# A group norm of the next layer computed inside attention windows: another form of it in the first layer, an earlier table of gather places, a later load of scan weights

## The chip, the core and the metric

The kernel runs on one core of a Trainium2 chip. The metric is the device time of one execution in microseconds (us). A core has five engines that run side by side and wait for each other by semaphores: PE (TensorE, matrix products), DVE (VectorE), ACT (ScalarE), POOL (GpSimd) and SP (SyncE, which here only issues transfers). Each engine takes its own instructions strictly in order. Transfers that SP and ACT issue run on 16 DMA engines. The profile also gives the clock that TensorE was granted, as a share of full speed.

## The reference

The input is a batch of 4 images of 256 channels on 64 x 64 places. Four layers follow each other, each of the form x = x + layer(gn(x)). The norm is `_gn`:

```python
g = v.reshape(B_, H_, W_, G, C_ // G)
m = jnp.mean(g, axis=(1, 2, 4), keepdims=True)
s = jnp.var(g, axis=(1, 2, 4), keepdims=True)
return ((g - m) / jnp.sqrt(s + eps)).reshape(v.shape)
```

It is called with x itself, so its last axis is the last image axis. With 64 places there and 32 groups, a group is two neighbouring columns of the image over all channels and rows. Layers 0 and 1 are the attention layers that this change touches. Each has two halves:

```python
y = mhsa(x, ...)          # 1x1 convolutions, tanh, then a recurrence h = f*h + (1-f)*z along one axis
return ssa(y_img, ...)    # attention in 8 x 8 windows
```

In `ssa`, each of the 64 windows of 64 places picks the four windows whose mean key fits its mean query best (`top_k`), takes their keys and values (`kv[idx]`), and attends to those 256 places with 8 heads. A 3 x 3 depthwise convolution of the values is added, and a 256 x 256 projection closes the layer. Layers 2 and 3 are state-space layers and are not touched.

## The kernel before, in words

The outer loop runs over the 4 images. For each, `attention_layers` runs layers 0 and 1, and two other functions run layers 2 and 3. The image x stays in SBUF as 128 partitions x (2 halves of the channels x 64 x 64 places). A strip is 8 columns of it, so there are 8 strips and each strip holds 4 norm groups.

Each attention layer has a scan phase and a window phase. **The scan phase** (`scan_phase`) goes through the 8 strips: it normalises a strip two strips ahead with `gn_four`, convolves, runs the recurrence, and stores keys and values of the strip to a table in DRAM (`kv_dram`; the values by `kv_dram<-vn`, L394, are the last part). It needs the layer's scan weights `att_wa` (1 MB, L115), and strips 0 and 1 must be normalised before it begins: for layer 1 that is done during the window phase of layer 0. `routing` then computes the four places of each window; the instruction on L472 writes them to the tile `idx`, which is the start of the window phase in this document.

**The window phase** (`window_phase`) takes the 64 windows in 32 pairs. There are 8 window phases in a run: images 0 to 3, and for each layer 0 and layer 1. Pair i goes through these steps:

- `gather(i)` fetches keys and values of the pair's 8 places by 8 transfers of 128 KB (L524). SP issues them, but ACT issues half of those of pairs 0 and 1. The buffers `kv` hold four pairs; `gather(i + 3)` stands at the end of pair i, after `values(i - 1)` has freed buffers.
- `indices(i)` loads the places into registers of the issuing engine: for pairs 0 to 3 straight from `idx` (L511, one load a window), for later pairs from `row` (L501, one load a pair).
- `load_row` stores `idx` to DRAM (`listed<-idx`, L493) and, when the store has landed, reads it back into one partition as `row` (L494). It stands behind `gather(2)` and `indices(3)`.
- `scores(i, h)` for h = 0, 1 (half of the heads) is 64 small products on PE (L546). `smallest` is a DVE reduction (L558), `exps` four ACT exponentials with their sums (L569), `normalise` a DVE reciprocal (L581) and four POOL multiplications of 128 x 256 (L584).
- `turn` transposes the result on PE (L597), `turned` copies it out on DVE and ACT (L608, L610), `values` multiplies with the values (L623), and `own_rows(i)` adds into the image of the convolution on DVE (L634). L634 runs once a pair, so its starts are used as marks of the pairs below.
- In two of four pairs the projection of the strip before is added to x (L644).

Other work is spread over the pairs by hand. `taps` are the last steps of the depthwise convolution on POOL, one a pair until pair 24: a multiplication into a tile `tap` (L254), then an addition (L257), in turn. `double` sends part of the queries to other partitions by SP (L309). Then there is the norm. The function `plan` puts its steps either into `mids[i]` (in the middle of pair i, ahead of `normalise(i, 0)`) or into `ends[i]` (at the end of pair i, behind everything else of it).

In layer 0 the steps are those of `gn`, for strips 0 and 1 of the next layer, begun at pairs 7 and 11:

1. `sums`, DVE, end of pair 7 (11), L143, and a product on PE at the end of pair 8 (12);
2. `center`, middle of pair 9 (13): the mean on DVE (L149), then POOL writes x minus the mean into `att_xn`, 128 x 1024 (L151);
3. `square`, ACT, end of pair 10 (14): L156, into the tile `gn_sq`, which has the tag "sq" with one buffer, and that is also the buffer of `tap`;
4. `reduce`, DVE, middle of pair 11 (15), L160, and a product at the end of it;
5. `scale`, middle of pair 12 (16): DVE adds the epsilon (L167), POOL raises to the power of minus a half (L168), and POOL multiplies `att_xn` by that, 128 x 1024 (L172).

In layer 1 the next layer needs only variances, so the steps are those of `stats`, for strips 0 to 6, begun at pairs 7, 11, 15 and so on: `sums` (L200), `mean` (L206), four ACT squares of 128 x 256 straight from x with mean and sum in the same instruction (L215, into a tile of the tag "xn"), a product, and `variance`, a DVE copy (L221).

`load_scan_weights(nxt)` stands, in layer 0, ahead of the loop over the pairs and behind `load_row`, in SP's order between `gather(2)` and `gather(3)`.

Of the kernel before, what the change touches and what calls it, by code (L numbers as in the profile page):

```python
# [8 lines left out]
F32 = mybir.dt.float32  # L9
# [3 lines left out]
ALU = mybir.AluOpType  # L13
# [5 lines left out]
P = 128  # L19
# [4 lines left out]
NW = 8  # L24
# [20 lines left out]
class Net:  # L45
# [33 lines left out]
    def attention_layers(self, x, w_drams, v_drams):  # L79
        tc, nc = self.tc, self.nc  # L80
        with ExitStack() as ctx:
# [31 lines left out]
            def load_scan_weights(lay):  # L113
                lay["wa"] = wp.tile([P, 2, 4 * C], F32, tag="wa", name="att_wa")
                nc.sync.dma_start(lay["wa"], lay["w"][:, :, 0 : 4 * C])  # L115
# [70 lines left out]
                return g[0], both(g[1], g[2]), both(g[3], g[4]), both(g[5], g[6])  # L186


            def stats(s, psum):
                xs = x.rearrange("p (c h w) -> p c w h", c=2, w=S)[:, :, strip[s], :]  # L190
                box = {}

                def columns(tag, part):
                    box[tag] = psum().tile([P, NT], F32, tag="mm", name=f"gn_{tag}")
                    nc.tensor.matmul(box[tag][:, 0:4], self.one_gn, part, start=True, stop=True)

                def sums():
                    box["s1"] = self.small.tile([P, 4], F32, tag="gn_s1", name="gn_s1")
                    xr = x.rearrange("p (n w) -> p n w", w=S)[:, :, strip[s]]
                    nc.vector.tensor_reduce(  # L200
                        box["s1"], xr.rearrange("p n (g t) -> p g n t", t=2), AX.XY, ALU.add
                    )

                def mean():
                    box["mean"] = self.small.tile([P, 4], F32, tag="gn_mean", name="gn_mean")
                    nc.vector.tensor_scalar(  # L206
                        box["mean"], box["pm"][:, 0:4], -1.0, None, ALU.mult
                    )

                def square(g):  # L210
                    if g == 0:
                        box["s2"] = self.small.tile([P, 4], F32, tag="gn_s2", name="gn_s2")
                        box["sq"] = norm.tile([P, 2, 8, S], F32, tag="xn", name="gn_sq")
                    two = slice(2 * g, 2 * g + 2)
                    nc.scalar.activation(  # L215
                        box["sq"][:, :, two], xs[:, :, two], AF.Square,
                        bias=box["mean"][:, g : g + 1], accum_out=box["s2"][:, g : g + 1],
                    )

                def variance():  # L220
                    nc.vector.tensor_copy(self.gvar[:, 4 * s : 4 * s + 4], box["pv"][:, 0:4])  # L221

                return (
                    sums, lambda: columns("pm", box["s1"]), mean,
                    *(lambda g=g: square(g) for g in range(4)),
                    lambda: columns("pv", box["s2"]), variance,
                )


# [247 lines left out]
            def window_phase(lay, work, psum, idx, nxt, taps):  # L477
                vec, wb = lay["vec"], lay["wb"]
                n_pair = NW * NW // 2
# [11 lines left out]
                def load_row():  # L491
                    listed = dram.tile([NW * NW, 8], U32, tag="listed", name="listed")
                    nc.sync.dma_start(listed, idx)  # L493
                    nc.sync.dma_start(  # L494
                        row.rearrange("o (s a) k -> o s a k", a=NW),
                        listed[:, 0:TOPK].rearrange("(o a s) k -> o s a k", o=1, a=NW),
                    )

                def indices(i):
                    if 3 < i < n_pair:  # L500
                        loads, win = nc.values_load_multi_w_load_instructions(  # L501
                            row[0:1, 2 * i : 2 * i + 2, :], engines=[ET.SP], min_val=0,
                            max_val=NW * NW - 1,
                            skip_runtime_bounds_check_because="places among 64 columns",
                        )
                        regs[i] = [win[0:TOPK], win[TOPK:]]
                    elif i < n_pair:
                        regs[i] = []
                        for w in range(2):
                            p = window(i, w)  # L510
                            loads, win = nc.values_load_multi_w_load_instructions(  # L511
                                idx[p : p + 1, 0:TOPK], engines=[queue(i, w)[1]], min_val=0,
                                max_val=NW * NW - 1,
                                skip_runtime_bounds_check_because="places among 64 columns",
                            )
                            regs[i].append(win)
# [121 lines left out]
                def project(s, m, psum):  # L638
# [10 lines left out]
                    return add  # L649

                indices(0)
                for i in range(3):
                    gather(i)
                    indices(i + 1)
                load_row()
                scores(0, 0)
                scores(0, 1)
                early = [query(lay, 5, m, psum, nc.vector, tag="pt", bufs=2) for m in range(2)]
# [5 lines left out]
                mids, ends, left = {}, {}, []  # L664

                def plan(steps, *where):
                    for f, (at, i) in zip(steps, where):
                        if i < n_pair:
                            at.setdefault(i, []).append(f)
                        else:  # L670
                            left.append(f)

                if nxt:
                    load_scan_weights(nxt)
                    for s in range(2):
                        i = 7 + 4 * s
                        plan(gn(nxt, s, lambda: psum), (ends, i), (ends, i + 1), (mids, i + 2),
                             (ends, i + 3), (mids, i + 4), (ends, i + 4), (mids, i + 5))
                else:

                    for s in range(NW - 1):
                        i = 4 * s + 7
                        plan(stats(s, lambda: psum), (ends, i), (ends, i + 1), (mids, i + 2),
                             (ends, i + 2), (mids, i + 3), (ends, i + 3), (mids, i + 4),
                             (ends, i + 4), (mids, i + 5))
                for i in range(n_pair):
                    sj, a = divmod(i, 4)
                    add = evict = None
                    exps(i, 0, (0, 1))
                    if i:  # L690
                        scores(i, 1)
                        turned(0, 0)
                        turned(0, 1)
                        turn(i - 1, 1)
                        smallest(i, 1)
                    exps(i, 0, (2, 3))
                    for t in mids.get(i, ()):
                        t()
                    if i == 0:
                        for f in early:  # L700
                            f()
                    normalise(i, 0)
                    if a == 3 and sj + 2 in (NW - 2, NW - 1):
                        evict = query(lay, sj + 2, 0, psum)
                    elif a == 0 and sj + 1 in (NW - 2, NW - 1):
                        evict = query(lay, sj + 1, 1, psum)
                    elif a in (1, 2) and sj:
                        add = project(sj - 1, a - 1, psum)
                    exps(i, 1, (0, 1))
                    scores(i + 1, 0)  # L710
                    if i:
                        turned(1, 0)
                        turned(1, 1)
                        values(i - 1)
                    turn(i, 0)
                    smallest(i + 1, 0)
                    exps(i, 1, (2, 3))
                    normalise(i, 1)
                    if i:
                        own_rows(i - 1)  # L720
                    for t in taps[i : i + 1]:
                        t()
                    if a in (0, 3) and i and dve_taps:
                        dve_taps.pop(0)()
                    if add:
                        add()
                    if evict:
                        evict()
                    gather(i + 3)
                    if a == 0 and 1 < sj + 1 < NW - 2:  # L730
                        double(sj + 1)
                    elif a == 1 and sj + 1 in (NW - 2, NW - 1):
                        double(sj + 1)
                    indices(i + 4)
                    for t in ends.get(i, ()):
                        t()
                turned(0, 0)
# [14 lines left out]
                box = {}  # L752
# [3 lines left out]
            with tc.tile_pool(name="at_p0", bufs=2, space=PSUM, reuse_waits="tile") as psum:  # L756
                box = {"psum": psum}
                g = [gn_four(layers[0], s, lambda: box["psum"]) for s in range(2)]
# [1413 lines left out]
```

## Time and profile before

| what | value |
|---|---|
| median of the runs | 11914.07 us (3 runs, 11912.61 to 11917.38) |
| the profiled execution | 11903.13 us, of which the span from first to last instruction 11901.3 us |
| PE busy | 10069.9 us, 85% |
| DVE busy | 9868.8 us, 83% |
| POOL busy | 8695.6 us, 73% |
| ACT busy | 7006.9 us, 59% |
| mean granted TensorE clock | 0.932 |
| the 8 window phases, end of the last instruction on L472 to the start of the last L634 | 274.2, 271.1, 268.1, 270.1 us in layer 0; 243.7, 245.1, 251.6, 252.6 us in layer 1 |

Busy shares over the whole span say little here, since some two thirds of the time lie in layers 2 and 3. What matters is where the window phases of layer 0 and of layer 1 differ. They do the same attention, in the same order; beside it they carry different norm work and, in layer 0, the weight load. The stretches that the next sections use are cut at starts of L634: "pair 9 to pair 16" is from its run for pair 9 to its run for pair 16.

### The profile page before, as it was taken

To read this page: it belongs to the slowest core of one execution; us is meant where nothing else is said; L and a number is where in the kernel's file an instruction comes from. 1 tells how busy PE (TensorE), PEld (TensorE's weight loads), DVE (VectorE), ACT (ScalarE), POOL (GpSimd) and SP (SyncE) were. 2 spreads that over 40 slices of the span, in tenths; PEclk is the share of its full clock that TensorE was granted. 3 is DMA by queue.
4 is the path that set the end of the run, shared out by engine and by line. 5 is a ranking of instruction groups with operands and counts; after the bars stand their busy time and mean duration, and the time that the engine had idled before them with its cause. 6 is when DMAs were issued, how large, how long until landed. Compare 5 with 4: busy or idle time off the path is not lost. (4 is left out here: it accounts for less than half of the span.)

```text
span 11901.3 us, 192225 instructions
## 1 busy us (share of the span) xinstructions
PE 10069.9 (85%) x71104; PEld 5762.7 (48%) x71104; DVE 9868.8 (83%) x8422; ACT 7006.9 (59%) x13096; POOL 8695.6 (73%) x5918
## 2 busy tenths in 40 slices
PE   8998887777899888777789988877778998887777
PEld 4564454444456455444445645544444564554444
DVE  6677998998767799899866779989987677998998
ACT  4565554776456555577645655557764565555776
POOL 4566886898456688689845668868984566886897
PEclk9998998999999899899999989989999998998998
DMA  3344454554334455455433445545543344554554
GB/s 96 101 133 137 173 178 144 171 181 159 89 99 137 138 172 175 147 169 181 157 88 101 133 139 172 176 147 169 181 158 92 98 134 139 173 175 145 169 175 154
DMA packets 682505, 1742.09 MB, mean 146 GB/s; under 512 B 88896, under 2 KB 194896, under 8 KB 681312
## 3 DMA queue, kind: packets, MB, share of 16 engines
q1 hardware_dynamic: 676448, 1721.41, 44.7%
q8 instruction: 563, 9.22, 0.3%
q10 hardware_dynamic: 5120, 8.39, 0.3%
q14 instruction: 374, 3.06, 0.1%
HBM read 1601.52 MB, written 94.39 MB: 142 GB/s over the span
## 5 line engine op out<-in xcount | busy, mean ns | idle before, releaser
L1016 POOL TENSOR_TENSOR hc<-h,cb 128x1024 f32<-128x1024 f32 x2056 | 4807.7, 2350 | 785.6 <-DVE h L1010 341.4
L1010 DVE TENSOR_TENSOR_SCAN h<-da,m_state,pb 128x1024 f32<-128x1024 f32 x1248 | 2920.2, 2340 | 163.1 <-DVE pb L1004 4.3
L962 PE MATMUL y<-ident,hc 128*128 128x128 f32 x16384 | 2345.2, 290 | 404.4 <-POOL hc L1016 333.7
L962 PEld LDWEIGHTS y<-ident,hc 128*128 128x128 f32 x16384 | 2043.7, 150 | 1127.6 <-POOL hc L1016 575.0
L1004 DVE TENSOR_TENSOR pb<-du,pb 128x1024 f32<-128x1024 f32 x1672 | 2024.4, 1211 | 118.9 <-PE pb L934 116.8
L946 ACT ACTIVATE da<-delta,m_v 128x1024 f32<-128x1024 f32 x1672 | 1899.4, 1141 | 135.7 <-DVE h L1010 118.9
L934 PE MATMUL pb<-m_parts,pick 128*128 128x512 bf16 x3312 | 1081.8, 411 | 835.0 <-DVE h L1010 768.7
L584 POOL TENSOR_SCALAR pr<-pr,sm,zero 128x256 f32<-128x256 f32 x2048 | 1136.1, 569 | 533.6 <-DVE sm L581 530.2
L569 ACT ACTIVATE pr<-sc,mn 128x256 f32<-128x256 f32 x2048 | 952.7, 477 | 552.4 <-DVE sm L581 359.9
L934 PEld LDWEIGHTS <-pick 128*128 128x128 bf16 x3312 | 264.0, 101 | 1779.8 <-DVE h L1010 977.2
L558 DVE TENSOR_REDUCE mn<-sc 128x4 f32<-128x1024 f32 x512 | 629.6, 1231 | 528.3 <-PE sc L546 527.0
L1010 DVE TENSOR_TENSOR_SCAN h<-da,pb 128x1024 f32<-128x1024 f32 x424 | 969.3, 2286 | 55.6 <-ACT m_u L1704 0.5
L920 POOL TENSOR_TENSOR bb<-du,bb 128x1024 f32<-128x1024 f32 x376 | 888.5, 2363 | 118.7 <-DMA bb<-m_cd 108.3
L597 PE MATMUL pt_ps<-ident,pr 128*128 128x128 f32 x4096 | 663.9, 297 | 85.0 <-POOL pr L584 40.2
L1010 DVE TENSOR_TENSOR_SCAN h<-dap,m_state,bb 128x1024 f32<-128x1024 f32 x288 | 672.2, 2334 | 65.9 <-ACT dap L946 46.1
L233 PE MATMUL conv_ps<-att_y,att_wb 128*128 128x512 f32 x1536 | 686.7, 597 | 3.0 <-DVE gvar L221 3.0
L546 PE MATMUL sc<-kv,q_swap 32*64 32x128 f32 x8192 | 599.4, 286 | 11.4 <-DMA kv<-kv_dram 8.8
L946 ACT ACTIVATE dap<-delta,m_v 128x1024 f32<-128x1024 f32 x376 | 419.8, 1116 | 308.5 <-DVE h L1010 245.8
L546 PE MATMUL sc<-kv,att_y 32*64 32x128 f32 x7168 | 580.1, 287 | 17.4 <-DMA kv<-kv_dram 13.7
L597 PEld LDWEIGHTS pt_ps<-ident,pr 128*128 128x128 f32 x4096 | 471.5, 148 | 225.6 <-POOL pr L584 138.4
L271 DVE SCALAR_TENSOR_TENSOR lp<-vimg,att_v,lp 128x512 f32<-128x512 f32 x672 | 507.7, 755 | 30.8 <-DVE lp L271 1.0
L546 PEld LDWEIGHTS sc<-kv,att_y 32*64 32x64 f32 x7168 | 434.0, 139 | 153.3 <-issue 58.8
(300 smaller groups left out, 17799.4 us busy)
## 6 DMA issues: line engine op xcount, KB each, us to landing
cb<-m_cd SPq DMA_DIRECT2D x2048, 512.0 KB, 3.8
kv<-kv_dram SPq DMA_DIRECT2D x1984, 128.0 KB, 2.8
bb<-m_cd SPq DMA_DIRECT2D x376, 512.0 KB, 5.5
kv_dram<-kst SPq DMA_DIRECT2D x128, 256.0 KB, 3.9
kv_dram<-vn SPq DMA_DIRECT2D x128, 256.0 KB, 4.1
q_swap<-att_y SPq DMA_DIRECT2D x96, 256.0 KB, 4.4
m_pe<-in_pe_dram SPq DMA_DIRECT2D x32, 512.0 KB, 4.5
out_dram<-yo SPq DMA_DIRECT2D x64, 256.0 KB, 2.4
```

The costliest lines, as they stand in the source:

```text
L233: nc.tensor.matmul(ps, w[:, k, w0 + m * P : w0 + (m + 1) * P], src[:, k], start=(k == 0), stop=(k == 1),)
L546: nc.tensor.matmul(sc[h][b * 64 : b * 64 + 64, r, w, m, :], (own(sj, m) if r == b else swap[sj % 2][:, m])[rows, 2 * a + w], kv[i, w][rows ...
L569: nc.scalar.activation(t[:, g].rearrange("p j r t -> p r j t"), sc[h][:, :, g // 2, g % 2, :].rearrange("p r (j t) -> p r j t", j=2), AF.E ...
L584: nc.gpsimd.tensor_scalar(t[:, g], t[:, g], s[:, g : g + 1], self.zero, ALU.mult, ALU.add)
L597: nc.tensor.transpose(pt[h][j][:, g, :], t[:, g, j].rearrange("p r t -> p (r t)"), self.ident,)
L920: nc.gpsimd.tensor_tensor(pb[i], slots[i][0]["du"], pb[i], ALU.mult)
L934: nc.tensor.matmul(pb[i][:, ss], self.pick[:, n : n + 1].to_broadcast([P, P]), blk["parts"][:, ss], start=True, stop=True,)
L946: nc.scalar.activation(da[i], blk["delta"], AF.Exp, scale=blk["a"](n))
L962: nc.tensor.matmul(blk["y"][:, ss], t[:, ss], self.ident, is_transpose=True, start=(n == 0 and ss.start % NT == 0), stop=(n == DS - 1 and ...
L1004: nc.vector.tensor_tensor(pb[i], blk["du"], pb[i], ALU.mult)
L1010: nc.vector.tensor_tensor_scan(h[i][:, ss], da[i][:, ss], pb[i][:, ss], state, ALU.mult, ALU.add)
L1016: nc.gpsimd.tensor_tensor(hc[i][:, ss], h[i][:, ss], cb[i][:, ss], ALU.mult)
```

## The change

It has three parts.

1. In layer 0 too, the norm of the next layer's strips 0 and 1 takes the steps of `stats`. Two steps are new: `deviation` (middle of pair 12 and 16) adds the epsilon on DVE and raises to the power on POOL, for 4 columns instead of 8; `scale`, twice, at the ends of pairs 13 and 14 (17 and 18), makes two POOL instructions of 128 x 256 each, (x + (minus mean)) * deviation, reading x and writing the tile that held the squares. That tile becomes `att_xn`. The steps of `gn` stay in use in the scan phases.
2. `load_row` moves ahead of `gather(0)`, in all 8 window phases, and pairs 2 and 3 take their places from `row` too.
3. `load_scan_weights(nxt)` moves to the end of pair 4, behind `gather(7)`, the query transfers (`double`) and `indices(8)`. In SP's order it is then directly ahead of `gather(8)`.

```diff
-            def stats(s, psum):
+            def stats(s, psum, lay=None):
...
                         box["sq"] = norm.tile([P, 2, 8, S], F32, tag="xn", name="gn_sq")
+                        if lay:
+                            lay["xn"][s] = box["sq"]
...
+                def deviation():
+                    rstd = self.small.tile([P, 8], F32, tag="gn_rstd", name="gn_rstd")
+                    box["rstd"] = rstd = rstd[:, 0:4]
+                    nc.vector.tensor_scalar(rstd, box["pv"][:, 0:4], 1e-5, None, ALU.add)
+                    nc.gpsimd.tensor_tensor(
+                        rstd, rstd, self.minus_half.to_broadcast([P, 4]), ALU.pow
+                    )
+
+                def scale(*gs):
+                    for g in gs:
+                        two = slice(2 * g, 2 * g + 2)
+                        nc.gpsimd.tensor_scalar(
+                            box["sq"][:, :, two], xs[:, :, two], box["mean"][:, g : g + 1],
+                            box["rstd"][:, g : g + 1], ALU.add, ALU.mult,
+                        )
...
-                    lambda: columns("pv", box["s2"]), variance,
+                    lambda: columns("pv", box["s2"]),
+                    *((deviation, lambda: scale(0, 1), lambda: scale(2, 3)) if lay else (variance,)),
...
-                    if 3 < i < n_pair:
+                    if 1 < i < n_pair:
...
                 indices(0)
+                load_row()
                 for i in range(3):
                     gather(i)
                     indices(i + 1)
-                load_row()
...
-                if nxt:
-                    load_scan_weights(nxt)
-                    for s in range(2):
-                        i = 7 + 4 * s
-                        plan(gn(nxt, s, lambda: psum), (ends, i), (ends, i + 1), (mids, i + 2),
-                             (ends, i + 3), (mids, i + 4), (ends, i + 4), (mids, i + 5))
-                else:
...
+                for s in range(2 if nxt else NW - 1):
+                    i = 4 * s + 7
+                    plan(stats(s, lambda: psum, nxt), (ends, i), (ends, i + 1), (mids, i + 2),
+                         (ends, i + 2), (mids, i + 3), (ends, i + 3), (mids, i + 4),
+                         (ends, i + 4), (mids, i + 5), (ends, i + 6), (ends, i + 7))
...
                     indices(i + 4)
+                    if i == 4 and nxt:
+                        load_scan_weights(nxt)
```

## The prediction

> **What bounds the kernel now.** I read the page first, then the sums by stretch for all 8 window phases, then the order of time of single engines. The page shows no engine that is full everywhere, so the stage decides. The change touches window phases alone, and layer 1 already does the norm in nearly the form that layer 0 is to get: it is the control. These are the sums by stretch from pair 9 to pair 16. The columns are start and end, length, the busy time of PE, weight load, DVE, ACT and POOL with counts, granted clock, DMA share and GB/s; first the four phases of layer 0, then the four of layer 1.
> ```profile
> 315.31:388.71 73.40, 62.42 (x1028) 47.31 (x1027) 40.39 (x63) 35.85 (x128) 48.43 (x68) 0.70 0.42 123
> 3283.76:3358.27 74.51, 65.73 (x1029) 50.12 (x1027) 39.83 (x64) 35.96 (x128) 48.52 (x68) 0.63 0.43 125
> 6260.69:6331.88 71.19, 57.31 (x1028) 43.43 (x1027) 40.94 (x63) 35.73 (x128) 48.33 (x68) 0.78 0.46 133
> 9232.42:9304.15 71.73, 57.83 (x1028) 43.57 (x1027) 40.56 (x63) 35.74 (x128) 48.33 (x68) 0.79 0.41 119
> 778.21:827.59 49.38, 46.86 (x1030) 34.93 (x1029) 38.35 (x63) 38.32 (x138) 38.85 (x63) 1.00 0.57 159
> 3745.38:3795.73 50.35, 47.09 (x1030) 35.91 (x1029) 38.46 (x64) 38.33 (x138) 38.84 (x63) 0.97 0.56 159
> 6725.88:6774.94 49.06, 45.42 (x1030) 34.35 (x1029) 38.44 (x64) 38.22 (x138) 38.85 (x63) 1.00 0.58 166
> 9694.36:9745.19 50.83, 47.57 (x1030) 36.09 (x1029) 38.27 (x63) 38.43 (x138) 38.82 (x63) 0.97 0.54 159
> ```
> The same seven pairs take 290.8 us in layer 0 and 199.6 in layer 1. No engine of layer 0 has 20 us more to do; POOL has 9.6 more. The rest is waiting, and a PE at 0.63 to 0.79 of its clock. In layer 1 PE is busy 95% of the stretch: there it is the bound. The order of time says where layer 0 waits, for ACT at pair 10, and for POOL at pair 12:
> ```profile
> 318.85 1.06 ACT L156 ACTIVATE gn_sq<-att_xn 128x1024 f32<-128x1024 f32 x1 [4.89 <-POOL vimg L257]
> ```
> ```profile
> 330.81 1.64 POOL L168 TENSOR_TENSOR gn_rstd<-gn_rstd,minus_half 128x8 f32<-128x8 f32 x1 [1.61 <-DVE sm L581]
> 332.53 1.90 POOL L172 TENSOR_TENSOR att_xn<-att_xn,gn_rstd 128x1024 f32<-128x1024 f32 x1
> 334.42 4.74 POOL L584 TENSOR_SCALAR pr<-pr,sm,zero 128x256 f32<-128x256 f32 x8
> ```
> First, the square waits 4.89 us until POOL's addition L257 has read `tap`: both tiles share the one buffer of the tag "sq". Behind the square stand all exponentials of the next pair. Second, power and multiplication (1.64 + 1.90) stand ahead of eight normalisations whose sums were ready. Both leave PE without transposes.
>
> The early part, pair 0 to pair 9, in the same columns: layer 0, then the first two phases of layer 1 (the other two took 67.52 and 64.55).
> ```profile
> 246.03:315.31 69.28, 63.72 (x1317) 48.43 (x1318) 45.62 (x74) 43.68 (x162) 51.13 (x82) 0.90 0.59 169
> 3215.72:3283.76 68.04, 62.23 (x1317) 46.62 (x1318) 45.45 (x73) 43.69 (x162) 51.19 (x82) 0.95 0.58 168
> 6195.40:6260.69 65.29, 60.54 (x1317) 45.41 (x1318) 45.28 (x73) 43.42 (x161) 50.63 (x82) 0.97 0.56 160
> 9162.23:9232.42 70.19, 63.55 (x1317) 48.34 (x1318) 45.48 (x74) 43.69 (x162) 51.13 (x82) 0.90 0.61 174
> 717.44:778.21 60.77, 57.30 (x1317) 43.12 (x1317) 45.53 (x73) 45.37 (x167) 48.22 (x81) 1.00 0.60 173
> 3684.03:3745.38 61.35, 58.43 (x1317) 43.55 (x1318) 45.24 (x73) 45.55 (x168) 48.66 (x81) 1.00 0.60 174
> ```
> Layer 0 loses 272.8 - 4 x 61.1 = 28.4 us here. Its cause shows on SP and PE in the first phase:
> ```profile
> 240.02 0.48 SPq L493 DMA_DIRECT2D listed<-idx  x1
> 241.69 0.82 SPq L494 DMA_DIRECT2D row<-listed  x1
> 242.57 0.40 SPq L115 DMA_DIRECT2D att_wa<-in_l_w_dram  x1
> ```
> ```profile
> 251.54 0.40 PE L546 MATMUL sc<-kv,att_y 32*64 32x128 f32 x2 [2.38 <-DMA kv<-kv_dram]
> ```
> `gather(3)` goes out behind store, readback and the 1 MB of weights, and its scores wait.
>
> **The norm.** Removed for each strip: POOL's L151 (2.47 us), L172 (1.90) and the power on 8 columns (1.64), DVE's reduction (1.22), one ACT square (1.06), and with them both stalls. Added: four ACT squares of 0.75 with 0.21 to read the sum, 3.84 in all; layer 1 carries exactly these at the same pairs, so they cost nothing beyond its stretch. The squares' tile has the tag "xn", so the 4.89 us wait goes away. If only the control's steps were left, layer 0 would gain 91.2 us. What the control lacks is `deviation` and `scale`.
>
> `deviation`: the DVE addition replaces a copy of 0.14 in the same place, no change. The power stands ahead of pair 12's normalisation on POOL, and behind it wait the normalisations, the tap and PE's transposes. In the control POOL begins that normalisation at 788.70, 0.15 after the deviation would be there, and ends at 790.86; the transposes start at 791.01. So of 1.64 us (the row of 8 columns; fewer columns may take less), 1.64 - 0.15 - 0.15 = 1.34 reach PE. The low end is 0.7, if the power is a third shorter and is partly caught up.
>
> `scale`: two POOL instructions at each of two pair ends. The contiguous form (L584, 128 x 256) takes 0.57. But x is read here at a step of 64 floats. The Trainium skill ("GPSIMD Engine Reference", section Performance pitfalls for Q7 kernels) says that a POOL read at a step over 8 bytes costs some 2.9 instead of 1.9 cycles an element; at its 1.2 GHz that is an estimate of 0.57 + 256 x 1.0/1.2 ns = 0.78. The row of POOL that reads x so, L151, speaks against it: 2.47 against 2.35 for a like two-input one (L1145), 5%, so 0.60. But two inputs may hide it, and ACT's squares of x take 0.75 where contiguous exponentials take 0.48 (L569). By the rule a step is 1.56, by the row 1.20; over 16 steps 6 us of POOL. I take 1.56. In the control POOL idles 0.49 ahead of pair 14's first normalisation and nothing ahead of pair 15's, and the transposes follow some 0.5 later: 0.6 and 1.0 reach PE. Together 2.94 a strip, 23.5 us for 8 strips. A gain is excluded, since this is work added to the control's chain; the low end is 6, the high end is below.
>
> **The clock.** The skill ("TensorE: Matmul & The Clock Gate", Part 1) has PE fall to half its clock after an idle window of about 3.4 us. By that, waits of 1 to 1.4 us cost their length. The trace is harsher: after the wait of 2.38 us at 251.54 the records show 0.50 from 253.1 on for 13.7 us. But in the control waits of about 0.6 us left it at 1.00. The new waits lie between. By the rule the sum above stands; by the row each strip adds one short half-clock spell, some 2.5 us, 20 in all. I take the rule for the sum, the row for the high end (43.5).
>
> Norm: -91.2 + 23.5 = -67.7 us.
>
> **The weights.** Taken away from `gather(3)`: -28.4, if this is all of the early loss. But they now stand directly ahead of `gather(8)`, behind 0.5 MB of queries. In the first phase of layer 1 SP begins `gather(8)` at 745.59, and PE its scores at 753.3, without a wait, and nothing to spare. In layer 0, from issue of the weights to the scores of the gather behind them, 242.57 to 253.0, it took 10.4 us for the two; so `gather(8)` would be there at about 755.8 (the weights out at 745.4), 2.5 late: the same wait, five pairs later. Before, such a wait cost 28.4/4 = 7.1 with the clock's loss; its bare length is 2.5. Pairs 7 to 9 take 7.2 to 7.8 us rather than 6.0, so the gathers catch up sooner: I take 5, in 4 phases +20. Net -8. Ends: 0 left of it (-28), or +7.1 each and no gain (0).
>
> **The table.** In all 8 phases SP now waits for the store's landing before the readback; behind that stand its half of `gather(0)` and all later gathers, and PE's first scores. SP already waits there for the landing of `kv_dram<-vn`, 16.7 us in 8 waits, 2.1 each; the store (0.48) and most of its landing (1.25 of waiting each time now) lie in that. What is left is the readback's issue, 0.8, on SP's half alone; PE waits for `gather(0)` already by 0.5 to 0.8 us in most phases of layer 0 and is ready at about the same time in layer 1. +0.8 x 8 = +6.4. Between 0 (ACT's half keeps the transfers busy meanwhile) and 1.3 x 8 = 10, if the store lands half a microsecond after the table. The later gathers gain 2 us of SP's time; layer 1 shows no wait at pair 3 that would be paid by it, so nothing. Two register loads of 0.31 become one of 0.53, nothing.
>
> **Sum.** -67.7 - 8.4 + 6.4 = -69.7 us. Against the profiled execution's 11903.1 that is 11833; the median of the runs is 10.9 above that one, so I name 11844.
>
> **Rivals.** (a) As summed, 11844: 0.57. (b) The new waits halve the clock, -91.2 + 43.5, the weights give nothing, the table takes 10: -38, 11876: 0.23. For it: the half clock at 253.1; against it: the control's 1.00. (c) POOL's additions vanish in its idle time and the weights hide: -91.2 + 6 - 28, and no cost of the table: -113, 11801: 0.12. For it: POOL is idle 10 of 49 us in the control; against it: not at the places where it counts. (d) The move doesn't take the stall away, because the square waits for some other reader: then rows 10 and 14, some 4.8 each, stay, 38 us: -32, 11882: 0.05. Against it: the same squares in layer 1 wait for no buffer. (e) Slower: the weights ahead of `gather(8)`. PE waits their whole 6 us and then stays at half clock to pair 16, some 60 us, at 40% more for each pair: 6 + 24 = 30 in each of 4 phases, 120 against the 68 + 28 - 6 gained: +30, 11944. It decides from 22 us a phase on. The longest half-clock stretch in a window phase so far is 27.3 us, so 0.03.
>
> The range reaches from (c) to a little beyond (b) and (d): 11802 to 11892. A measurement tells about 0.2%, 24 us, from no change: faster 0.91, within 0.06, slower 0.03.
>
> **What would show it.** The stretch from pair 9 to 16 at 50 to 56 us in layer 0, at a clock near 1; no wait of `gn_sq` for L257; the new POOL instructions at 0.6 to 0.8; the wait for `kv` gone from pair 3 and there at pair 8; `gather(0)` of SP 0.8 later. I am wrong if pair 8 costs over 10 us, if the power or the scales cost a strip over 6, or if the stretch keeps its 70.

## The result and the profile after

The changed kernel takes 11822.36 us (median of 4 runs, 11818.24 to 11830.95) against 11915.72 before (4 runs, 11912.61 to 11921.65): a ratio of 0.9922, interval 0.9905 to 0.9939, so 93 us less, between 73 and 113. Its profiled execution took 11825.03 us with a span of 11823.2, which is 78.1 less than the span before: the window phases of layer 0 take 89.4 less, those of layer 1 4.2 more, and all the rest 7.1 more.

These are the sums by stretch of the kernel after, from pair 9 to pair 16, in the columns of the prediction: four phases of layer 0, then two of layer 1.
```profile
311.74:363.25 51.51, 48.06 (x1028) 36.68 (x1027) 37.09 (x62) 37.62 (x136) 44.13 (x69) 0.93 0.59 166
3272.31:3322.56 50.25, 45.82 (x1028) 34.09 (x1027) 37.13 (x61) 37.51 (x136) 44.08 (x69) 1.00 0.57 161
6223.50:6275.05 51.55, 48.08 (x1028) 36.61 (x1027) 37.14 (x62) 37.60 (x136) 44.12 (x69) 0.93 0.59 168
9179.73:9231.23 51.50, 48.53 (x1028) 36.87 (x1027) 37.03 (x62) 37.73 (x136) 44.12 (x69) 0.93 0.60 169
753.83:811.03 57.20, 53.74 (x1030) 42.18 (x1029) 38.29 (x63) 38.43 (x138) 39.08 (x63) 0.82 0.57 160
3716.64:3765.49 48.85, 45.89 (x1030) 34.66 (x1029) 38.35 (x63) 38.21 (x138) 39.15 (x63) 1.00 0.55 157
```
Layer 0 has come down from 290.8 to 204.8 us, to where layer 1 stands, and its clock from 0.63-0.79 up to 0.93-1.00. Into the 57.20 in layer 1 fell a half-clock spell of 20.5 us. Such spells (times in which the records show a clock of 0.50) come and go, and so the sum of the same four stretches in layer 1, whose norm is the same before and after, ran from 196.8 to 213.4 us over all profiles of this study. That is the yardstick for sums of four stretches; differences under some 15 us in one of them carry no weight alone. Stretches without any half clock repeat far better: of the eight such phases of layer 0 in the changed kernel and in the runs that have its norm in place, seven took 50.1 to 50.3 us and one 51.1.

On POOL, in order of time, in the first phase of layer 0 around pairs 13 and 14 (lines have moved: L603 is the normalisation, L236 the new scale):
```profile
335.35 0.78 POOL L273 TENSOR_SCALAR tap<-vimg,att_v,zero 128x512 f32<-128x512 f32 x1
336.11 1.55 POOL L236 TENSOR_SCALAR gn_sq<-x,gn_mean,gn_rstd 128x256 f32<-128x256 f32 x2
337.64 2.18 POOL L603 TENSOR_SCALAR pr<-pr,sm,zero 128x256 f32<-128x256 f32 x4
...
343.74 1.56 POOL L236 TENSOR_SCALAR gn_sq<-x,gn_mean,gn_rstd 128x256 f32<-128x256 f32 x2
```
The scale takes 1.55 for two, as summed (1.56), and the normalisation follows without a gap. Behind the second two scales stand eight normalisations in a row, and PE waits for one of them at pair 15:
```profile
345.26 4.81 POOL L603 TENSOR_SCALAR pr<-pr,sm,zero 128x256 f32<-128x256 f32 x8
```
```profile
347.97 0.77 PE L616 MATMUL pt_ps<-ident,pr 128*128 128x128 f32 x5 [0.67 <-POOL pr L603]
```
Here, at 350.0, a half-clock spell of 6.8 us begins. The third and fourth phases have one at the same pair; they take 51.5 us, where the second, which has none, takes 50.25.

Of the wait that the norm took away, the list of waits of the kernel before has the whole (total, times and longest, in us); the kernel after has no such row:
```profile
ACT gn_sq L156 <- POOL vimg L257: 38.9, 8, 4.9
```

The early stretches, pair 0 to pair 9, of layer 0 went from 272.8 to 259.6 us:
```profile
247.79:311.74 63.95, 60.27 (x1317) 45.56 (x1318) 45.52 (x72) 45.49 (x167) 48.52 (x81) 0.95 0.63 179
3207.18:3272.31 65.13, 60.06 (x1317) 45.38 (x1317) 45.42 (x72) 45.48 (x167) 48.50 (x81) 0.95 0.63 178
6156.64:6223.50 66.86, 60.62 (x1317) 45.76 (x1318) 45.51 (x74) 45.80 (x168) 48.97 (x81) 0.95 0.61 173
9116.05:9179.73 63.68, 60.17 (x1317) 45.11 (x1317) 45.26 (x74) 45.89 (x168) 49.07 (x81) 0.97 0.65 185
```
Pairs 1 to 3 take 18 us in all four phases (19.5 to 26.3 before), but the two pairs after pair 5, which hold the scores of pair 8, take 15.8 to 19.0 us; 12.9 is their length without a wait (12.9 to 15.2 before). In the third phase PE waits there for keys, and SP, shown for the first phase, has the weights ahead of that gather:
```profile
6194.85 0.40 PE L565 MATMUL sc<-kv,att_y 32*64 32x128 f32 x2 [2.20 <-DMA kv<-kv_dram]
```
```profile
272.99 2.12 SPq L328 DMA_DIRECT2D q_swap<-att_y  x2
275.94 0.40 SPq L115 DMA_DIRECT2D att_wa<-in_l_w_dram  x1
276.59 12.79 SPq L543 DMA_DIRECT2D kv<-kv_dram  x16
```

### The profile page after: what moved, and what is told of

It reads as the page before. It is cut to its first block, busy times and chain, and to the rows that moved or that the text cites. A ratio compares the mean times of both kernels' runs of the same rounds, so it can differ in the third digit from the quotient of the medians.

```text
span 11823.2 us, 191837 instructions
## 1 busy us (share of the span) xinstructions
PE 9992.3 (85%) x70632; PEld 5736.4 (49%) x71104; DVE 9857.6 (83%) x8414; ACT 7021.4 (59%) x13152; POOL 8687.6 (73%) x5934
## 5 line engine op out<-in xcount | busy, mean ns | idle before, releaser
L947 PE MATMUL pb<-m_parts,pick 128*128 128x512 bf16 x2840 | 971.0, 412 | 827.9 <-DVE h L1023 767.0
L603 POOL TENSOR_SCALAR pr<-pr,sm,zero 128x256 f32<-128x256 f32 x2048 | 1143.7, 575 | 475.4 <-DVE sm L600 472.5
L565 PE MATMUL sc<-kv,q_swap 32*64 32x128 f32 x8192 | 585.8, 281 | 13.8 <-DMA kv<-kv_dram 6.9
L565 PE MATMUL sc<-kv,att_y 32*64 32x128 f32 x7168 | 565.3, 281 | 18.1 <-DMA kv<-kv_dram 12.9
L565 PEld LDWEIGHTS sc<-kv,att_y 32*64 32x64 f32 x7168 | 421.6, 136 | 149.1 <-ACT pr L588 54.4
```

The costliest lines, as they stand in the source:

```text
L565: nc.tensor.matmul(sc[h][b * 64 : b * 64 + 64, r, w, m, :], (own(sj, m) if r == b else swap[sj % 2][:, m])[rows, 2 * a + w], kv[i, w][rows ...
L603: nc.gpsimd.tensor_scalar(t[:, g], t[:, g], s[:, g : g + 1], self.zero, ALU.mult, ALU.add)
L947: nc.tensor.matmul(pb[i][:, ss], self.pick[:, n : n + 1].to_broadcast([P, P]), blk["parts"][:, ss], start=True, stop=True,)
```

## The experiments

My theory: the norm brings nearly all, by taking two stalls out of pairs 10 to 16; the weights only carry their stall to another pair; the table costs a little. The rivals: the additions on POOL vanish, or the transfers brought the gain. Ratios are to the kernel before, timed on the same chip, with 95% intervals. "Early", "middle" and "late" are the four stretches of layer 0 from pair 0 to 9, 9 to 16 and 16 to 31; "start" is from the end of L472 to L634 of pair 0. All are sums over four phases in us, from the one profile of each run.

| run | ratio | start | early | middle | late |
|---|---|---|---|---|---|
| before | 1 | 101.4 | 272.8 | 290.8 | 418.4 |
| after | 0.9922 (0.9905-0.9939) | 107.5 | 259.6 | 204.8 | 422.2 |
| norm alone | 0.9929 (0.9915-0.9942) | 100.9 | 273.8 | 204.7 | 422.9 |
| table alone | 0.9989 (0.9982-0.9995) | 105.5 | 254.9 | 288.7 | 420.1 |
| weights alone | 1.0002 (0.9994-1.0010) | 100.3 | 274.3 | 289.1 | 416.5 |
| norm and table | 0.9918 (0.9905-0.9932) | 104.2 | 255.0 | 210.2 | 421.6 |
| own buffer | 0.9958 (0.9943-0.9974) | 103.5 | 266.5 | 246.2 | 420.9 |
| no additions | 0.9918 (0.9903-0.9933) | 111.0 | 259.3 | 191.5 | 431.3 |
| split and late | 0.9920 (0.9906-0.9933) | 100.9 | 254.0 | 207.2 | 420.3 |
| weights late | 0.9922 (0.9908-0.9935) | 110.0 | 245.8 | 206.1 | 423.5 |
| late scales | 0.9918 (0.9905-0.9932) | 108.5 | 262.9 | 191.7 | 429.1 |
| table behind | 1.0010 (1.0004-1.0017) | 102.6 | 272.2 | 286.6 | 413.4 |
| table, direct loads | 0.9984 (0.9976-0.9993) | 108.6 | 256.7 | 290.4 | 413.9 |
| all three | 0.9940 (0.9927-0.9954) | 103.9 | 274.8 | 196.5 | 434.0 |

**Norm alone.** The changed kernel with parts 2 and 3 undone.
```diff
-                    if 1 < i < n_pair:
+                    if 3 < i < n_pair:
...
-                load_row()
                 for i in range(3):
                     gather(i)
                     indices(i + 1)
+                load_row()
...
+                if nxt:
+                    load_scan_weights(nxt)
...
-                    if i == 4 and nxt:
-                        load_scan_weights(nxt)
```


> The new norm alone; table and weights stay where they were. My sum: -67.7 us against before (a ratio near 0.9943), the four stretches of layer 0 from pair 9 to 16 at 50 to 56 us, the early stretches of layer 0 unchanged at 273 in all. Rival, that POOL's additions vanish in its idle time: -85 (0.993), the stretches within 1 us of layer 1's 50. Rival, that transfers brought the gain: the stretch shrinks, but the run gains under 40 us (over 0.9967).

0.9929 of 11906 us: 85 us less (69 to 101), the middle at 204.7 as in the changed kernel, the early stretches unchanged. The norm brings nearly all of the gain; table and weights beside it (0.9922) are not apart from nothing. The time agrees with the rival's -85 better than with my -67.7, which lies just outside the interval.

**Table alone.** The kernel before with part 2.
```diff
-                    if 3 < i < n_pair:
+                    if 1 < i < n_pair:
...
                 indices(0)
+                load_row()
                 for i in range(3):
...
-                load_row()
```


> The table's store and readback ahead of the first gathers, alone. My sum: +6 us, from SP's half of gather(0) going out 0.8 us later in each of 8 window phases, the wait for the fourth pair's keys unchanged. Rival: the store and readback no longer stand between gather(2) and gather(3), so weights and gather(3) go out some 2 us sooner, the wait of layer 0 at pair 3 shrinks from 2.4 us to under 1, and the early stretches of layer 0 lose 15 us: -9 in all. From stalls in pair 9 to 16 no change in either.

13 us less (6 to 21): my sign was wrong, the rival holds. The early stretches lose 18 us, though the start takes 4 more. SP in the first phase, in order of time:
```profile
223.89 0.80 SPq L494 DMA_DIRECT2D row<-listed  x1
225.10 14.40 SPq L524 DMA_DIRECT2D kv<-kv_dram  x16
240.13 0.40 SPq L115 DMA_DIRECT2D att_wa<-in_l_w_dram  x1
240.73 4.27 SPq L524 DMA_DIRECT2D kv<-kv_dram  x6
```
`gather(3)` goes out at 240.73, 20.1 us after the places are known, where it took 21.9 before (243.19 with the places at 221.3), and PE has no wait for keys at pair 3 in that phase. Over the four phases it goes out 19.8 us after the places on average, 21.8 before; 18.7, 18.2, 21.1 and 21.9 us go into pairs 1 to 3, from 26.3, 22.3, 19.5 and 26.0.

**Weights alone.** The kernel before with part 3.
```diff
                 if nxt:
-                    load_scan_weights(nxt)
                     for s in range(2):
...
                     indices(i + 4)
+                    if i == 4 and nxt:
+                        load_scan_weights(nxt)
```


> The weights' load behind pair 4's index load, alone. My sum: -8 us: the wait for keys at pair 3 of layer 0 is gone (-28 with its half clock), one of 2 to 3 us stands at pair 8 instead (+20). Rival: the stall only moves, pair 6 to 8 take as much as pairs 1 to 3 gave, 0. Rival: the weights hide wholly at the new place, -28. The early stretches of layer 0 from pair 0 to 9 at 265, 273 or 244 us in all.

No difference that can be told, and early stretches of 274.3: the second expectation, the stall only moves. PE, in the order of time of the first phase, waits at pair 8 what it had waited at pair 3:
```profile
287.24 0.65 PE L546 MATMUL sc<-kv,att_y 32*64 32x128 f32 x2 [2.56 <-DMA kv<-kv_dram]
```
The two pairs there take 17.4, 21.0, 17.4 and 16.9 us; over 12.9 each that is 21 us, just the +20 of my sum (they had stood 5.5 over it before, so the rise is 16). What failed is the other side: pairs 1 to 3 gave back 13 us instead of 28. Store and readback still stood ahead of `gather(3)`, which went out 21.1 us after the places on average, only 0.7 sooner than before.

**Norm and table.** The changed kernel with the weights at their old place.
```diff
+                if nxt:
+                    load_scan_weights(nxt)
...
-                    if i == 4 and nxt:
-                        load_scan_weights(nxt)
```


> The changed kernel with the weights back at their old place behind gather(2). My sum: 8 us slower than the changed kernel, with the wait for keys at pair 3 again and none at pair 8. Rival: the move is worth nothing beside the other two parts, the same time within 3 us, since the earlier table has already taken the wait at pair 3 away.

0.9918 beside 0.9922: the move of the weights is worth nothing that can be told beside the other two, and the early stretches (255.0) are not above those of the changed kernel (259.6).

**Own buffer.** The kernel before, the squares in a buffer of their own, rounded to bf16.
```diff
-                    box["sq"] = norm.tile([P, 2, 8 * S], F32, tag="sq", name="gn_sq", bufs=1)
+                    box["sq"] = norm.tile([P, 2, 8 * S], BF16, tag="gsq", name="gn_sq", bufs=1)
```


> The kernel before, with one edit: the squares of the old norm go to a buffer of their own, which fits only in bf16, so they are rounded to bf16. If the 4.89 us wait of the square is for the buffer it shares with the tap, pairs 10 and 14 fall from 11 to about 6.5 us in layer 0, 8 x 4.5 = 36 us less, with perhaps 8 more from pairs 11 and 15 where the tap waited in its turn. Rival (d) of the prediction, another reader: no change. Half of the norm's gain should remain unreached in pairs 12 and 16, which power and multiplication on POOL lengthen.

The wait for L257 is gone, the middle falls by 44.6 us of the 86 that the new norm takes away, the time by 50 (31 to 68). Square and reduction take 1056 and 1219 ns as before, so the rounding itself brings no time: about half of the norm's gain is the shared buffer alone, with the old steps of the norm. Rival (d) of the prediction falls. Pairs 10 and 14 take 6.4 to 8.1 us instead of 11.0. Pairs 12 and 16 stay at 13.4 to 14.5, where the run of the norm alone has 7.7 to 8.3: the second stall is all there, with power and multiplication ahead of eight normalisations as before:
```profile
324.95 1.65 POOL L168 TENSOR_TENSOR gn_rstd<-gn_rstd,minus_half 128x8 f32<-128x8 f32 x1 [0.23 <-DVE sm L581]
326.67 1.90 POOL L172 TENSOR_TENSOR att_xn<-att_xn,gn_rstd 128x1024 f32<-128x1024 f32 x1
328.56 4.74 POOL L584 TENSOR_SCALAR pr<-pr,sm,zero 128x256 f32<-128x256 f32 x8
```
That these two instructions make the second stall is read from such lines; no run takes them away alone.

**No additions.** The changed kernel without `deviation` and `scale`: strips 0 and 1 of layer 1 then hold squares instead of normalised values.
```diff
-                    *((deviation, lambda: scale(0, 1), lambda: scale(2, 3)) if lay else (variance,)),
+                    variance,
```


> The changed kernel without deviation and scale: a copy of the variance stands in their place as in layer 1, so strips 0 and 1 of layer 1 get squares in place of normalised values. What the two new steps cost on the path. My sum: 23.5 us less than the changed kernel. By the changed kernel's own stretches (204.8 against 199.6, and 422.2 against 418.4 later): 9 us less. Rival, wholly hidden: no difference beyond 3 us.

The middle falls by 13.3 us, but the late stretch rises by 9.1, and the ratio (0.9918) is not apart from the changed kernel's. The rise is half clock: 23.9 us of it fell into the four late stretches of this profile, 6.8 into those of the changed kernel. In the middle no phase has any, and all four take 47.8 to 48.0 us, against 50.2 with the additions and without half clock. So the additions cost 2.4 us a phase, 10 in all, not 23.5, and some 4 more by the three spells at pair 15. The pairs show where: 12 and 16 take 0.5 more each and 15 takes 1.4 more, while pairs 18 and 19, with the second strip's scales, take 0.1 more at most. The times alone can't tell it from nothing.

**Weights late.** The weights at pair 18.
```diff
-                    if i == 4 and nxt:
+                    if i == 18 and nxt:
```


> As the changed kernel, with the weights' load at pair 18 alone. If the waits at pair 8 come from the weights: 14 us less than the changed kernel, pair 6 of layer 0 back at 6.1 us. Rival: no change, because layer 1 has such waits too without any weights.

With the weights late, pairs 6 and 7 of three phases of layer 0 are back at 13.0 us and the early stretches at 245.8, 13.8 less than in the changed kernel, as expected. So the weights caused those waits. Against the kernel before, the early stretches are 27.0 less, nearly the whole 28.4 that the prediction counted as early loss: earlier table and harmless weights together take it away. But beside the changed kernel it doesn't show in the time: 0.9922, the same.

**Split and late.** As the last one, with only the store ahead of `gather(0)` and the readback behind it.
```diff
-                def load_row():
+                def store_row():
...
+                def load_row(listed):
...
                 indices(0)
-                load_row()
+                listed = store_row()
                 for i in range(3):
                     gather(i)
+                    if i == 0:
+                        load_row(listed)
...
```


> The changed kernel with the weights' load at pair 18 rather than pair 4, and the readback of the table between gather(0) and gather(1), the store staying ahead of gather(0). Gather(22), the one behind the weights there, has some 4 us to spare. If the waits at pair 8 come from the weights, the early stretches of layer 0 fall from 260 to 246 us, and SP's half of gather(0) goes out as in the kernel before: 14 + 5 us less than the changed kernel. Rival: the waits at pair 8 come from the query transfers and stay, 0 to 5 us less.

The start of layer 0 is back at 100.9, and the early stretches are 8.2 longer again; 0.9920 is not apart from the changed kernel's 0.9922. None of the hoped-for 19 us shows in the time.

**Late scales.** The changed kernel with power and scales, one POOL instruction each, at the ends of pairs 25 to 30.
```diff
+                def power():
...
-                    *((deviation, lambda: scale(0, 1), lambda: scale(2, 3)) if lay else (variance,)),
+                    *((deviation, power, *(lambda g=g: scale(g) for g in range(4))) if lay else (variance,)),
...
-                         (ends, i + 4), (mids, i + 5), (ends, i + 6), (ends, i + 7))
+                         (ends, i + 4), (mids, i + 5),
+                         *((ends, 25 + s + p) for p in (0, 1, 2, 3, 4)))
```


> The changed kernel with POOL's power and its four multiplications a strip moved to the ends of pairs 25 to 30, one instruction a pair end, where no tap is left on POOL; the DVE addition stays. If these steps cost what the run without them says, the stretch from pair 9 to 16 of layer 0 goes from 204.8 back to about 192 in all and the late stretch stays at 422: 10 to 13 us less than the changed kernel. Rival, that they only stand in for stalls that come anyway: no difference, the late stretch takes what the middle gives.

The middle falls to 191.7, as foreseen, again with 47.8 to 48.2 us a phase and no half clock. The late stretch takes 6.9 back, with 23.9 us of half clock in it, as much as in the run without the additions, which has no scales there. The ratio is that of the run without the additions, and not apart from the changed kernel's.

**Table behind.** The kernel before with `load_row` behind `gather(3)`.
```diff
-                load_row()
...
                     gather(i + 3)
+                    if i == 0:
+                        load_row()
```


> The kernel before with store and readback of the table moved the other way, behind gather(3) at the end of pair 0; weights stay ahead of gather(3). It tells why the earlier table gained. If it gained by leaving the place ahead of the weights and gather(3): the early stretches of layer 0 fall from 273 to about 255 us here too, and without the 4 us that the wait ahead of gather(0) costs from the places to the first pair (101 us in layer 0 as before): -15 to -18 us. Rival, that being ahead of gather(0) is what helps, by sparing the direct register loads: the stretches stay at 273, no gain.

No gain; rather 12 us lost (5 to 20). Both expectations fail: the stretches are the rival's, but its reason isn't, as the next run shows. In layer 0 the wait has moved one pair on. SP, then PE, in the first phase:
```profile
246.28 0.54 SPq L493 DMA_DIRECT2D listed<-idx  x1
250.28 0.81 SPq L494 DMA_DIRECT2D row<-listed  x1
253.36 2.60 SPq L524 DMA_DIRECT2D kv<-kv_dram  x4
```
```profile
261.83 0.65 PE L546 MATMUL sc<-kv,att_y 32*64 32x128 f32 x2 [2.73 <-DMA kv<-kv_dram]
```
Here the readback goes out 4.0 us after the store, with a gather and the weights ahead of it; `gather(4)` waits for that and for the readback. At both places between gathers that were tried, the gather behind pays for the round trip. Where the 12 us lie isn't shown: layer 0's stretches are 8.6 us shorter in sum than before, the early ones of layer 1 rose from 254.2 to 268.0, but the profiled execution, at 11902.67, was one of the run's two fastest.

**Table, direct loads.** The table alone, with the direct register loads of pairs 2 and 3 kept.
```diff
                 indices(0)
+                load_row()
...
-                load_row()
```


> The table ahead of gather(0) as in the run of the table alone, but pairs 2 and 3 still take their places from idx by the direct register loads. It parts the two halves of that edit, after the table behind gather(3) brought nothing. If what counts is that SP's store and wait leave the stream of gathers for the time in which SP waits for the values' landing anyway: the early stretches of layer 0 at 255 again, -10 to -15 us. Rival, that sparing four direct register loads of 0.31 us for two of 0.53 is what helps: the stretches at 273, no gain.

19 us less (8 to 29), early stretches of 256.7: the order alone does it, not the register loads.

**All three.** The late scales, with the table behind `gather(3)` and the weights at pair 18.
```diff
...
-                    if 1 < i < n_pair:
+                    if 3 < i < n_pair:
...
-                load_row()
...
+                    if i == 0:
+                        load_row()
...
-                    if i == 4 and nxt:
+                    if i == 18 and nxt:
```


> The new norm with late scales, the table behind gather(3), the weights at pair 18. If the parts add up: the early stretches of layer 0 at 246, the middle ones at 192, from the places to the first pair 101: 30 us less than the changed kernel, a ratio near 0.990 of the kernel before. Rival, that half-clock spells come at other places instead: within 10 us of the changed kernel.

0.9940, with early stretches of 274.8 (its profiled execution, 11848, is the slowest of its five). The expected 30 us did not come; it looks as if the table at that place takes back what it and the weights gave elsewhere, but the ratio is not apart from the changed kernel's. No version tried is faster than the changed kernel by more than the intervals; the lowest medians, 11802 and 11804, are those of norm and table and of late scales.

## Why the prediction was right, point by point

The time, 11822, lies in the range, 22 below the forecast of 11844 and as far above rival (c) at 11801; the time alone doesn't choose between them. That the forecast came so near is in part luck: its three terms were off by 17, 19 and 8 us, and the last error ran against the other two. By its parts:

- **The two stalls of the norm.** Right. The square did wait for the buffer (38.9 us of waits gone, and the run with an own buffer), and the stall at pairs 12 and 16 went with the old steps on POOL. Layer 1 was a fair control, though it stood 8.1 us too high: without the additions layer 0 takes 191.5, not 199.6. The control had some half clock (0.97 in two phases), and from pair 15 on it carries steps of a third strip.
- **"2.94 a strip, 23.5 us for 8 strips".** Mis-sized. The new steps cost 10 us at full clock and some 14 with the half-clock spells that follow them in the profile. The durations were nearly right (0.79 us for a multiplication, 0.78 taken from the Trainium skill's rule on strided reads, "GPSIMD Engine Reference", section Performance pitfalls for Q7 kernels, and not the 0.60 that L151 suggested; the power on 4 columns 1.02 us instead of 1.64). What was wrong is how much reaches PE: the power lengthens pairs 12 and 16 by a half of a microsecond, not by 1.34; the scales lengthen pair 15 by 1.4, near the 1.6 of the sum, but the second strip's, at pairs 18 and 19, by 0.1 at most. I let each delay on POOL arrive at PE less one gap, and for both strips alike. Why the second strip's scales cost nothing is open.
- **"The later gathers gain 2 us of SP's time; layer 1 shows no wait at pair 3 that would be paid by it, so nothing".** This step failed, and with it the sign of the table's term: +6.4 forecast, -13 measured. I looked for the payer in layer 1 and had booked layer 0's wait at pair 3 wholly to the weights. The 2 us were right (`gather(3)` goes out 19.8 instead of 21.8 us after the places), but the wait of layer 0 has two causes: the round trip delays the issue of `gather(3)`, and the weights, 1 MB, go out ahead of it. Taking away either shortens it. At the start SP's half of `gather(0)` goes out 5.0 us after the places instead of 3.7, on the average of all 8 phases, the upper end of what was forecast. What of it reaches the first pair differs: layer 0's start grows by 3 to 10 us in the seven runs with the table ahead of `gather(0)`, where the runs with the old place differ by 3 among themselves; that of layer 1 does not grow (105.0 to 109.8, 108.5 before).
- **The weights, -8.4.** Measured 0 alone, and 0 beside the table. The stall at pair 8 was right in place and in price (21 against 20); the gain at pairs 1 to 3 was half of what I had counted, for the reason above.
- **The clock.** Taking the skill's rule ("TensorE: Matmul & The Clock Gate", Part 1) for the sum was right in effect: of the 20 us of the high end some 4 came. But that was not for the rule's reason: half-clock spells do follow waits far under 3.4 us, as told below, and of the 20 phases of all runs that have the scales at pair 15, seven have one begin there, of the 12 without scales there none; there the measurement decides.
- **Sum.** Norm -85 measured for -67.7, table -13 for +6.4, weights 0 for -8.4: -98 in parts, -93 together. The norm was 17 under, the table 19 under, the weights 8 over. For the norm alone rival (c), -85, was the better forecast. The table and the weights together were forecast at -2; singly they brought -13, and beside the norm 8 (0.9922 against 0.9929), which is not clear of noise.

What stays open: whether weights at pair 18 or late scales are worth 5 to 14 us, as their stretches say, or nothing, as the times say. Half-clock spells, which fall at other pairs in every profile, may hide it.

## What to carry to other kernels

When a side step stalls a tuned loop, look first for the tile tag it shares with another engine's scratch: here a buffer of 4 KB a partition held back ACT for 4.9 us at a time, and a buffer of its own was worth half of what the whole new norm brought. A transfer that must go through one queue costs where the consumer behind it has no slack; moving it only helps if the slack at the new place is known, and a store that is waited for stood best, of the places tried, where its queue waits already. When one wait has two causes in series, cost the removal of each with the other in place.

## What the runs showed of the hardware that was not expected

TensorE's half clock began without any long idle stretch. In the first layer-0 phase of the kernel after, the records show 0.50 for 6.8 us from 350.0 on; in the 3.4 us before, PE was idle 0.88 us in all, and its longest wait in the 6.8 us before was 0.67. In the third phase of layer 1 a spell of 17.1 us followed 1.36 us of idle in 3.4, the longest wait 1.33. So small gaps that sum to a quarter of that time can be enough, while the single wait of 0.54 us at 252.73 left the clock at 1.00. They need not be: in the same profile PE was idle for 1.25 of the 3.41 us from 6818.59 on, and the clock stayed at 1.00. What decides it is open.

The readback of the table goes out when its 2 KB store has landed. That took 1.7 us from the store's issue where it stood behind `gather(2)` in the first phase (240.02 to 241.69), and 4.0 us behind 1 MB of weights and `gather(3)` (246.28 to 250.28). In that last run the four phases of layer 0 show 2.9 to 4.2 us, and those of layer 1, with `gather(3)` but no weights ahead, 2.1 to 2.4. The store is the same, so its landing went by what lay ahead of it.
